# Starting the experts of the first ten chunks 36 edge tiles after their sums instead of 60, in a graph layer with a mixture of experts

## The chip, the core and the metric

The kernel runs on one core of one Trainium2 chip. The metric is the device time of one execution in microseconds. The core has five engines with a queue of instructions each: TensorE (PE in the profile; PEld is its loading of weights, which overlaps), VectorE (DVE), ScalarE (ACT), GpSimd (POOL) and SyncE (SP). An engine takes its instructions strictly in the order of the program, and waits when the next one needs something that isn't there yet.

## The reference

6,250 nodes with 256 features, 100,000 edges sorted by target. A graph layer adds to every node a linear map of itself and of the mean of its neighbours. Then a mixture of experts follows: 8 experts of 256-512-256, each node goes to the 2 with the highest scores.

```python
h = layernorm(x)
msg = segment_sum(h[src], dst); deg = segment_sum(1, dst)
x = x + concat([h, msg / max(deg, 1)]) @ W.T + b
xn = layernorm(layernorm(x)) * gamma + beta
logits = xn @ Wr + br;  top 2 of 8, w = softmax(top_vals)
for e in range(8):
    y += (gelu(xn @ W1[e] + b1[e]) @ W2[e] + b2[e]) * w_full[..., e]
x = x + y
```

## The kernel before

**Edges.** The edges are cut into 784 *edge tiles* of 128 edges. 14 tiles make a *window*, whose targets lie within 128 nodes; four windows (56 tiles) make a *chunk*; there are 14 chunks. For a tile, POOL gathers 128 rows of the transformed neighbours by an indirect DMA (L601, into 28 buffers `xg`, so that it can be 28 tiles ahead), DVE writes 0/1 matrices for half a window at a time (`hot`, L612), and PE multiplies the two and sums in PSUM (`pS`, L618). At a window's end ACT keeps a copy of the sums (`keep_sums`, L640), and DVE makes the nodes' new features of them (`window_x1`, L658 to L660).

**From sums to experts.** When the four windows of a chunk are done, a chain of small steps leads to its experts: DVE and ACT make the norms and the routing, PE counts the tokens of each expert (`count_tokens`, L678, which waits for DVE's `both`, L672), DVE writes matrices that sort the tokens (`one_hot_slots`, L697 and L698), PE sorts them (L705) and ACT takes them out of PSUM (L708). DVE works out where each expert's run of tokens goes (`share_runs`, `place_rest`, `place_runs`; the last result is `runs_i`, L780). Then ACT copies the runs into the experts' input `xe` in 32 copies (`copy_runs`, L859, 8 groups of 4). `find_rows` (a matmul at L809, then DVE to L822) makes a plan of where each node will find its results, and SP writes it to DRAM in four small DMAs (`put_plan`, L826) and reads back what is complete (`load_plans`, L841).

**Experts.** A chunk's experts are 16 *tasks* on PE: 8 of the first layer (`hidden`, L884, 16 recorded matmuls each, followed by 8 GELUs on ACT, L889) and 8 of the second (`result`, L897, 8 recorded matmuls each, followed by an addition on DVE, L901, and a DMA). Every first-layer task reads `xe`, and so waits for all of the chunk's copies. Tokens beyond 128 of an expert go to extra tiles, which are done once in each of three batches of chunks (chunks 1 to 8, 9 to 13, 14; `more_stages`, L927 to L945). When a batch is done, its nodes' results are gathered from DRAM (POOL, L976), weighted and added (DVE, L983) and written out.

**Who sets the order.** All of this is one stream, written out by hand. After each edge tile, `after` (L1085) issues what is due at that tile, and then tasks from a list: each task has a cost in the text (2.0 for a first-layer, 1.75 for a second-layer task), and a tile may spend 0.72 (0.6 in the last chunk). A chunk's 16 tasks cost 30, so they are spread over 42 tiles. What is due when is said by a class of offsets, counted in tiles from the chunk's last edge tile (`window_done`, L1014). There are three such classes, `Steps` (L993), `LateSteps` (L999) and `LastSteps` (L1005). Before the change chunks 1 to 10 use `Steps`, chunks 11 to 13 `LateSteps`, and chunk 14 `LastSteps`:

| step, offset in tiles | Steps | LateSteps |
| --- | --- | --- |
| features of the last window (x1) | 2 | 2 |
| norms, routing, choices | 9, 11, 16 | 7, 9, 13 |
| count | 19 | 15 |
| sorting matrices, from and to | 22, 28 | 17, 22 |
| sorting on PE, from and to | 26, 32 | 19, 25 |
| runs, rest, place | 30, 33, 36 | 20, 22, 24 |
| the 8 groups of copies, from and to | 40, 50 | 26, 34 |
| find_rows | 46 | 28 |
| put_plan, from and to | 47, 53 | 29, 32 |
| load_plans | 56 | 34 |
| experts start | 60 | 36 |

Offsets 1 to 56 are the tiles of the next chunk, 57 to 112 those of the chunk after it. So with `Steps` a chunk's tasks lie at offsets 60 to 102, inside the chunk after next, and with `LateSteps` at offsets 36 to 78, at the end of the next chunk and the start of the one after it.

Of the kernel before, what the change touches and what calls it, by code (L numbers as in the profile page):

```python
# [22 lines left out]
CW = 4  # L23
# [3 lines left out]
LATE = 40  # L27
XG = 28
RAW = 1
LATE_CHUNKS = 4  # L30


@with_exitstack
def gnn_ffn_kernel(ctx: ExitStack, tc: tile.TileContext, x, x_cols, src, dst, dst_next, gw, gw_t, gb, gb_cols, gamma, beta,
# [42 lines left out]
    W = src.shape[1]  # L77
# [545 lines left out]
    def take_raw_sums(V):  # L623
        V.raw = work.tile([P, D], F32, name="raw", bufs=1)
        nc.scalar.activation(V.raw, V.pS[:, :D], AF.Copy)
# [366 lines left out]
    now, spent, clock, due, added, spares = None, 0.0, 0.0, 0.0, 0.0, 0  # L992
    class Steps:  # L993

        x1, var, roots, norms, route, exps, weigh, choices, count = 2, 5, 7, 9, 11, 14, 15, 16, 19
        hot, sort = (22, 24, 26, 28), (26, 28, 30, 32)
        runs, rest, place, tiles, copied, rows, pace, start, apart = 30, 33, 36, 39, 40, 46, 1.5, 60, 2

    class LateSteps:  # L999

        x1, var, roots, norms, route, exps, weigh, choices, count = 2, 4, 5, 7, 9, 11, 12, 13, 15
        hot, sort = (17, 18, 20, 22), (19, 21, 23, 25)
        runs, rest, place, tiles, copied, rows, pace, start, apart = 20, 22, 24, 27, 26, 28, 1.25, 36, 1

    class LastSteps:  # L1005

        x1, var, roots, norms, route, exps, weigh, choices, count = 2, 4, 5, 6, 7, 8, 9, 10, 12
        hot, sort = (13, 14, 17, 18), (15, 16, 19, 20)
        runs, rest, place, tiles, copied, rows, pace, start, apart = 15, 16, 19, 24, 21, 22, 1, 29, 1

    def at(t, f, *args):
        later.setdefault(max(t, now), []).append(lambda: f(*args))

    def window_done(V, G, K, t):  # L1014

        i = V.g - K.first
        S = LastSteps if K.first + CW == W else LateSteps if K.first + LATE_CHUNKS * CW >= W else Steps
        G.x1.append(V.x1)
        more = 0
        if V.g < RAW:  # L1020
            take_raw_sums(V)
            at(t + 1, turn_raw_sums, V)
            at(t + 3, multiply_raw_sums, V)
            more = 4
        if V.g < W - 1:
            at(t + more, keep_sums, V)
        at(t + S.x1 + more, window_x1, V)
        at(t + S.x1 + more, statistics, G.mv[:, i, :], V.x1[:, :D])
        if i < CW - 1:
            return  # L1030
        at(t + S.var, variances, G)
        at(t + S.roots, roots, G)
        at(t + S.norms, norms, G, work)
        at(t + S.norms, logits, G)
        at(t + S.route, route, G, work)
        at(t + S.exps, exps, G)
        at(t + S.weigh, weigh, G, work)
        at(t + S.choices, choices, G)
        at(t + S.count, count_tokens, G, K)
        G.one_hot = [None] * CW  # L1040
        for m in range(CW):
            at(t + S.hot[m], one_hot_slots, G, m)
            at(t + S.sort[m], sort_tokens, G, m)
        at(t + S.runs, share_runs, K)
        at(t + S.rest, place_rest, K)
        at(t + S.place, place_runs, K)
        at(t + S.tiles, tile_experts, K)
        for e in range(NX):
            at(t + S.copied + int(e * S.pace), copy_runs, K, e)
        at(t + S.rows, find_rows, K)  # L1050
        for m in range(CW):
            at(t + S.rows + 1 + m * S.apart, put_plan, G, m)
        at(t + S.rows + 2 + CW * S.apart, load_plans, K)
        at(t + S.start, start_experts, K)
# [61 lines left out]
    for index in range(W // CW):  # L1116
        K = Group()
# [9 lines left out]
        for g in range(K.first, K.first + CW):  # L1127
            if g > 0:
                V = V_next
            for c in range(C):  # L1130
                t = g * C + c
                add_edges(V, c)
                if c == 0:
                    hot_tiles(V, HC)
                if c == HC and g + 1 < W:
                    V_next = new_window(g + 1, V)
                if t + XG < len(edge_tiles):
                    gather(*edge_tiles[t + XG])
                for to, what in loads[:1]:
                    loads.pop(0)  # L1140
                    nc.sync.dma_start(to, what)
                if u_tasks and t % 2 == 0:
                    u_tasks.pop(0)()
                    if not u_tasks:
                        u_pools.close()
                        slots = fast_pools.enter_context(tc.tile_pool(name="slots", bufs=2))
                        at(t + 60, load_last)
                        xe = slots.tile([P, KD, SC], F32, name="xe", bufs=1)
                        for n in range(4):
                            at(t + 3 + 5 * n, clear_slots, n)  # L1150
                        w1_sb, w2_sb, parts = weights(slots)
                        for n, (to, what) in enumerate(parts):
                            at(t + 2 + 2 * n, nc.scalar.dma_start, to, what)
                if c == HC + 5:
                    load_u(V)
                if c == C - 1:
                    window_done(V, G, K, t)
                after(t)
# [12 lines left out]
    with tc.If(wrong_r > 0), tc.tile_pool(name="gp", bufs=1) as gp:  # L1171
# [9 lines left out]
        with tc.For_i(0, W * C) as j:  # L1181
# [16 lines left out]
            count = gp.tile([P, 1], F32, name="count")  # L1198
# [113 lines left out]
```

## Time and profile before

| | |
| --- | --- |
| three timed runs | median 1427.65 us (1426.55 to 1431.58) |
| the profiled execution's own time | 1418.08 us |
| its span, first to last instruction | 1416.3 us |
| first edge tile starts, last one ends | 101.0 and 1255.8 us |
| mean granted clock of TensorE | 0.892 of full speed |
| POOL's gather of one edge tile (L601) | 0.951 us mean, and 0.30 us until the next at its fastest |

Times in the profile are microseconds from the start of the span. A timeline line gives start, length, engine, line of the code, operation, tiles, how many instructions were merged (xN), and in brackets the idle time of the engine before it and what ended that. A line by stretches gives for each engine its busy time and, in parentheses, its instructions, then the granted clock of TensorE, the DMAs' share and their rate. One matmul of the text appears as two records, since the numbers are float32.

### The profile page before, as it was taken

The page shows a single profiled execution, that of the slowest core. Times are in us where ns is not written, and L with a number is a line of the kernel's source. Part 1 is how long each engine was busy: PE and PEld are TensorE (multiplying, and loading weights), DVE is VectorE, ACT ScalarE, POOL GpSimd, SP SyncE. Part 2 cuts the span into 40 slices and gives each one's busy share as a digit, 9 for nine tenths or more (in the row PEclk, how much of TensorE's full clock was granted, in tenths as well). Part 3 has the DMA queues.
Part 4 walks back from the last instruction along what each step waited for, and adds up shares of the span by engine and source line. Part 5 has one row for each costly group of instructions (what it writes and reads, how often), then busy time and mean ns, then how long its engine had stood idle before and what let it go on. Part 6 is the DMA issues. An engine that isn't in the chain of part 4 may idle for free. (4 is left out here: it accounts for less than half of the span.)

```text
span 1416.3 us, 18881 instructions
## 1 busy us (share of the span) xinstructions
PE 1123.6 (79%) x5352; PEld 903.0 (64%) x5352; DVE 690.8 (49%) x2433; ACT 460.5 (33%) x1281; POOL 843.9 (60%) x892
## 2 busy tenths in 40 slices
PE   7819957696987879698796969899889897986760
PEld 6718734575766758586675857567767786774650
DVE  6637776163444435354443534555462643656423
ACT  3310003333342333344243323433542343532310
POOL 0256666666666666666666666566656666564543
PEclk9859977898998989899897988999999998997876
DMA  9858895445454454544445454454545453564754
GB/s 331 285 181 269 270 324 157 104 123 122 114 128 113 114 120 117 123 122 120 118 115 112 123 119 115 118 124 115 120 111 133 116 134 103 115 197 139 197 148 126
DMA packets 143578, 210.08 MB, mean 148 GB/s; under 512 B 36652, under 2 KB 111128, under 8 KB 143340
## 3 DMA queue, kind: packets, MB, share of 16 engines
q0 software_dynamic: 42768, 118.91, 34.3%
q1 hardware_dynamic: 92364, 80.45, 18.0%
q10 hardware_dynamic: 8336, 9.45, 2.0%
q8 instruction: 45, 0.74, 0.2%
q14 instruction: 65, 0.53, 0.1%
HBM read 163.86 MB, written 44.86 MB: 147 GB/s over the span
## 5 line engine op out<-in xcount | busy, mean ns | idle before, releaser
L601 POOL DMA_INDIRECT xg<-z_d,src_i x770 | 732.5, 951 | 415.2 <-issue 175.7
L618 PE MATMUL pS<-xg,hot 128*128 128x265 f32 x1568 | 452.4, 418 | 68.8 <-DVE hot L612 33.4
L618 PEld LDWEIGHTS pS<-xg,hot 128*128 128x128 f32 x1568 | 304.8, 204 | 151.7 <-issue 97.5
L884 PE MATMUL ph<-xe,w_sb 128*128 128x128 f32 x1792 | 255.4, 293 | 75.5 <-issue 66.3
L884 PEld LDWEIGHTS ph<-xe,w_sb 128*128 128x128 f32 x1792 | 243.1, 207 | 94.8 <-issue 77.4
L612 DVE TENSOR_TENSOR hot<-cols,rel 128x896 f32<-128x896 f32 x112 | 121.9, 1089 | 275.5 <-PE pS L618 154.3
L897 PE MATMUL py<-w_sb,hid 128*128 128x256 f32 x896 | 223.2, 391 | 28.0 <-issue 16.8
L889 ACT ACTIVATE hid<-ph,b_sb 128x128 f32<-128x128 f32 x448 | 126.4, 374 | 270.4 <-remote 125.5
L897 PEld LDWEIGHTS py<-w_sb,hid 128*128 128x128 f32 x896 | 172.2, 195 | 64.5 <-issue 36.4
L859 ACT ACTIVATE xe<-xs x448 | 139.3, 311 | 86.3 <-issue 36.4
L976 POOL DMA_INDIRECT xg<-y_d,plans x98 | 95.7, 977 | 83.1 <-issue 21.4
L901 DVE TENSOR_TENSOR rows<-py,b_sb 128x512 f32<-128x512 f32 x56 | 38.5, 688 | 168.9 <-PE py L897 62.7
L708 ACT ACTIVATE xs<-pm,beta_sb,gamma_sb 128x256 f32<-128x256 f32 x112 | 57.2, 566 | 169.2 <-PE pm L705 73.7
L705 PE MATMUL pm<-to,xn 128*128 128x256 f32 x224 | 62.5, 403 | 24.6 <-DVE to L698 18.7
L640 ACT ACTIVATE sums<-pS 128x265 f32<-128x265 f32 x55 | 21.4, 389 | 172.1 <-PE pS L618 100.2
L705 PEld LDWEIGHTS pm<-to,xn 128*128 128x128 f32 x224 | 44.1, 201 | 35.6 <-issue 11.6
L271 PE MATMUL ph<-gc,x_t 128*128 128x264 f32 (+1 forms) x200 | 58.8, 420 | 8.2 <-ACT root L180 4.2
L889 ACT ACT_TABLE_LOAD x25 | 32.1, 1283 | 77.8 <-PE pS L618 43.5
L271 PE MATMUL pm<-gc,x_t 128*128 128x264 f32 (+1 forms) x192 | 54.9, 411 | 0.0
L271 PEld LDWEIGHTS ph<-gc,x_t 128*128 128x128 f32 x200 | 40.2, 205 | 18.6 <-ACT root L180 4.6
L983 DVE SCALAR_TENSOR_TENSOR xg<-xg,plans,xg 128x256 f32<-128x256 f32 (+1 forms) x98 | 45.4, 482 | 12.5 <-DMA xg<-y_d,plans 10.9
L660 DVE SCALAR_TENSOR_TENSOR x<-pS,rdeg,x 128x264 f32<-128x264 f32 x55 | 27.1, 493 | 48.1 <-DMA x<-u_d 35.4
(214 smaller groups left out, 873.4 us busy)
## 6 DMA issues: line engine op xcount, KB each, us to landing
y_d<-rows SPq DMA_DIRECT2D x56, 256.0 KB
xg<-z_d,src_i POOLq DMA_INDIRECT x770
w_sb<-w_dram ACTq DMA_DIRECT2D x16, 512.0 KB
x<-u_d SPq DMA_DIRECT2D x55, 132.0 KB
x_d<-x SPq DMA_DIRECT2D x55, 128.0 KB
u_d<-u_t SPq DMA_DIRECT2D x24, 264.0 KB
x_t<-x_cols_dram SPq DMA_DIRECT2D x12, 512.0 KB
xu<-x_dram SPq DMA_DIRECT2D x24, 256.0 KB
```

What stands on the lines that cost most here:

```text
L271: nc.tensor.matmul(pz, x_t[:, t, k, :], gc[:, h * KD + k, :n], start=(k == 0), stop=(k == KD - 1))
L601: nc.gpsimd.indirect_dma_start(out=xg[(g * C + c) % XG][:, :DZ], out_offset=None, in_=z_d[:, :], in_offset=bass.IndirectOffsetOnAxis(ap=sr ...
L612: nc.vector.tensor_tensor(hot, col[:, None, :].to_broadcast([P, HC, P]), V.rel[:, c:c + HC, None].to_broadcast([P, HC, P]), op=ALU.is_equal)
L618: nc.tensor.matmul(V.pS, V.hot[c // HC][:, c % HC, :], xg[(V.g * C + c) % XG], start=(c == 0), stop=(c == C - 1))
L705: nc.tensor.matmul(px[:, k, :], G.xn[i][:, k * P:(k + 1) * P], G.one_hot[i], start=True, stop=True)
L708: nc.scalar.activation(xs[:, at:at + 2 * P], px[:, k, :], AF.Identity, bias=beta_sb[:, k:k + 1], scale=gamma_sb[:, k:k + 1])
L859: nc.scalar.activation(xe[:, :, bass.ds(to_at, CAP)], src[:, :, bass.ds(src_at, CAP)], AF.Copy)
L884: nc.tensor.matmul(ph[:, i, a * SH:(a + 1) * SH], w1_sb[:, U.e + a, k, c * P:(c + 1) * P], xe[:, k, at:at + SH], start=(k == 0), stop=(k = ...
L889: nc.scalar.activation(U.hid[:, c, a * SH:(a + 1) * SH], ph[:, i, a * SH:(a + 1) * SH], AF.Gelu, bias=b1_sb[:, U.e + a, c:c + 1])
L897: nc.tensor.matmul(U.py[:, h, :], U.hid[:, c, h * P:(h + 1) * P], w2_sb[:, U.e + h, c, :], start=(c == 0), stop=(c == KH - 1))
L976: nc.gpsimd.indirect_dma_start(out=V.y2[r], out_offset=None, in_=y_d[:K.batch.end_row, :], in_offset=bass.IndirectOffsetOnAxis(ap=plans[:c ...
L983: nc.vector.scalar_tensor_tensor(V.o, V.y2[r], plans.bitcast(F32)[:count, n, 2 + r:3 + r], V.o, op0=ALU.mult, op1=ALU.add)
```

## The change

The class `Steps` takes over the offsets of `LateSteps`, which goes, with the constant that chose between them. So chunks 1 to 10 go through the same steps as chunks 11 to 13 do; chunks 11 to 14 keep theirs. No instruction's shape changes, and the number of matmuls, gathers, DVE instructions and DMAs stays the same.

```diff
-LATE_CHUNKS = 4
...
     class Steps:
-        x1, var, roots, norms, route, exps, weigh, choices, count = 2, 5, 7, 9, 11, 14, 15, 16, 19
-        hot, sort = (22, 24, 26, 28), (26, 28, 30, 32)
-        runs, rest, place, tiles, copied, rows, pace, start, apart = 30, 33, 36, 39, 40, 46, 1.5, 60, 2
-
-    class LateSteps:
-
         x1, var, roots, norms, route, exps, weigh, choices, count = 2, 4, 5, 7, 9, 11, 12, 13, 15
         hot, sort = (17, 18, 20, 22), (19, 21, 23, 25)
         runs, rest, place, tiles, copied, rows, pace, start, apart = 20, 22, 24, 27, 26, 28, 1.25, 36, 1
...
-        S = LastSteps if K.first + CW == W else LateSteps if K.first + LATE_CHUNKS * CW >= W else Steps
+        S = LastSteps if K.first + CW == W else Steps
```

## Prediction

> **What bounds the kernel now.** I read first the busy times, then the stretches of the edge chunks, then the timelines of PE, ACT and DVE around one chunk's way from its sums to its experts.
>
> ```profile
> PE 1123.6 (79%) x5352; PEld 903.0 (64%) x5352; DVE 690.8 (49%) x2433; ACT 460.5 (33%) x1281; POOL 843.9 (60%) x892
> ```
>
> PE is the fullest engine, and it is the one that every edge tile and every task goes through in order. POOL is no bound: gathers start 1.25 us apart at the fastest (0.95 and 0.30), so 56 need 70 us, and PE's list of waits has only 1.7 us for a gather in the whole edge phase. So the time is PE's work plus PE's standing still. The stretches of chunks 8 and 9 (`Steps`), 12 and 13 (`LateSteps`):
>
> ```profile
> 667.20:750.60 83.40, 68.87 (x334) 56.03 (x334) 37.66 (x134) 30.58 (x86) 53.10 (x57) 0.91 0.48 117
> 750.60:832.60 82.00, 68.34 (x335) 56.41 (x335) 37.82 (x135) 28.61 (x80) 53.37 (x57) 0.90 0.48 119
> ...
> 1008.70:1096.60 87.90, 76.83 (x399) 64.59 (x399) 38.92 (x136) 31.95 (x90) 54.95 (x59) 0.94 0.48 120
> 1096.60:1179.50 82.90, 74.33 (x407) 62.36 (x406) 38.26 (x135) 33.09 (x94) 51.68 (x55) 0.96 0.47 120
> ```
>
> A usual chunk has 334 PE records, 69 us busy, 82 to 83 us long: 14 us idle, at a granted clock of 0.9. The late chunks look better (9 to 11 us idle, clock 0.95), but they hold 65 and 73 records more, because a backlog of tasks leaves PE no tile without one. So they are not yet proof of what `LateSteps` does to chunks with nothing left over.
>
> Where the 14 us go in a usual chunk, by PE's timeline:
>
> ```profile
> 826.71 2.05 PE L618 MATMUL pS<-xg,hot 128*128 128x265 f32 x8
> 832.56 3.48 PE L618 MATMUL pS<-xg,hot 128*128 128x265 f32 x8 [3.80 <-issue]
> 835.83 2.24 PE L884 MATMUL ph<-xe,w_sb 128*128 128x128 f32 x16
> ...
> 841.67 0.27 PE L884 MATMUL ph<-xe,w_sb 128*128 128x128 f32 x1 [1.83 <-issue]
> 843.78 0.37 PE L884 MATMUL ph<-xe,w_sb 128*128 128x128 f32 x1 [1.84 <-issue]
> 845.89 0.60 PE L884 MATMUL ph<-xe,w_sb 128*128 128x128 f32 x2 [1.73 <-issue]
> ```
>
> Some 3.8 us go at tile 56, where PE has raced through tiles without tasks and DVE's next `hot` ends only at 832.5. The larger part is a *crawl* from 839 to 852: single matmuls 0.7 to 1.8 us apart with no semaphore missing, 9 us lost. It comes again in chunks 3 to 10, each time while SP writes the plan (here 831 to 846) and POOL issues gathers back to back. It does not come beside the `LateSteps` plans at 1060, 1144 and 1227 (at most single gaps of a microsecond), when PE had tasks all along. Its cause I can't read from the trace.
>
> **The change, step by step.** The cycle of a usual chunk is the time from one start of experts to the next. First matmuls of L884 are at 253.4 (chunk 1) and 835.8 (chunk 8): seven cycles of 83.2 us. I build the new cycle from three legs and compare.
>
> *Leg 1, start of experts (offset 36) to the chunk's end (56).* 21 tiles at 0.46 us (two records of 0.225 apart) are 9.7; by 0.72 a tile, six first-layer tasks (1.78 each at full clock, from 1216.82 to the next start in PE's timeline of chunk 14's edges) and two second-layer ones (1.72, from 1221.55) fall here, 14.1; two joins of windows (L621, 0.55) 1.1. Together 24.9. As PE has stood still before, I add 2: after 3.80 us idle above, 8 records took 3.48 us instead of 2.05. Leg 1 is 27.
>
> The Trainium skill ("TensorE: Matmul & The Clock Gate", the table "Why this matters for your kernels") says that gaps over about 3 us bring the array back to half clock, and this speaks against gathering the idle time in one place. The row above agrees; by the page's window of 3.4 us the loss would be about 1.7 us an occurrence (an estimate), against the 2 that I take from the row.
>
> *Leg 2, the chunk's end to count (offset 15).* PE's own work is 17.4 (14 tiles 6.4, four second-layer and two first-layer tasks 10.4, one join), but the chain sums, x1, norms, routing, choices is longer: in chunks 11, 12 and 13 the first L678 started 21.2, 22.5 and 25.1 us after the chunk's last edge matmul (at 1030.15, 1117.58, 1204.80). I take their mean, 22.9. This is shorter than 39 us in chunk 8 (746.7 to 786.1), which has the crawl in it and four tiles more.
>
> *Leg 3, count to start (offset 36).* DVE needs count, four pairs of sorting matrices and some 35 small steps up to `runs_i`; in chunk 13 that went from 1205.9 to 1221.6 nearly without a pause. ACT then does 32 copies, all of which the first expert matmul waits for. In chunk 13, ACT and PE (two timelines):
>
> ```profile
> 1222.38 1.34 ACT L859 ACTIVATE xe<-xs  x4
> ...
> 1234.73 1.34 ACT L859 ACTIVATE xe<-xs  x4 [0.41 <-ACT xe L859]
> ```
> ```profile
> 1204.80 0.69 PE L678 MATMUL pm<-both,ones 128*128 128x64 f32 x2 [4.73 <-DVE both L672]
> ...
> 1236.12 2.05 PE L884 MATMUL ph<-xe,w_sb 128*128 128x128 f32 x16 [0.91 <-ACT xe L859]
> ```
>
> That is 31.3 us, 13.7 of it copies, and PE waited only 0.9 because tasks were left over from before. In chunks 2 to 8 after the change the last task is issued at about offset 20, so PE has 21 tiles (9.7), sorting (four times 0.87), two second-layer tasks (3.4), count, plan and join (1.8): 18.4 us of work in a leg of 31.3. **It will stand still 13 us in front of the first L884.** In the old order the same wait hardly shows, since 41 tiles and most tasks lie between count and start.
>
> Cycle: 27 + 22.9 + 31.3 and 0.8 for small waits for `rows` and `hid` (the 0.5 to 1.2 us a chunk of now) = 82.0, against 83.2, if there is no crawl. *The crawl* is the unknown. It costs 0 to 10 us (late chunks, chunk 9). The plan is now written from about 18 us after count on; POOL, refilling for the tiles that PE races through, is back to back just then. Most of it falls in PE's wait; what outlasts that, or slows ACT's copies, counts. I take 3, nearer to the late rows. Cycle 85.0; seven cycles cost 7 x 1.8 = **+12.6**.
>
> SP's queue: behind the plan's writes stand `load_plans`, the next x1's store and the next load of `u_d`. Moved from offsets 47 to 56 to 29 to 34, they no longer hold up the chunk's last x1, which now comes 18 us late after the crawl and comes 3.6 to 8.8 us after the end in chunks 11 to 13; that is in leg 2 already. POOL and DVE get no more instructions; nodes of the first batch are gathered 24 tiles earlier, and end before the last chunk in both.
>
> *Around the cycles.*
> - Chunk 1's experts start earlier: its count is held by DVE at 208.6 (13.1 us of wait in the trace) and will be; plus 31.3 is 239.9 instead of 253.4. **-13.5.** The weights are issued by 222 at the latest, and hide.
> - From the start of chunk 8's experts on there are 24 more tiles to go: 24 x 0.46 = **+11.0**; the crawl of chunk 9 (9.1 us of gaps) moves in front of that start: **-9.1**.
> - Batch 1's extra tiles keep PE in tasks until about tile 693. Then chunks 12 and 13 meet an empty list before their start, which they don't now (today's backlog ends where they start): 13 and about 7, **+20**.
> - Two tasks of each kind (7.0 us) come ahead of the last edge tile instead of behind it. From 1256 on PE's gaps before its last matmul add up to 37 us, so I count half as saved there: 7.0 - 3.5 = **+3.5**.
>
> Sum: 12.6 - 13.5 + 11.0 - 9.1 + 20 + 3.5 = +24.5. On the profiled execution's 1418.1 that is 1442.6; the median of the timed runs stands 9.6 above it, and I add the same 24.5 to it: **1452 us**.
>
> **Rivals.**
> 1. *The late rhythm without crawl and with a shorter chain (faster).* With few tasks in leg 3, DVE and ACT are less disturbed, and idle PE costs nothing where POOL refills. For it: no crawl in three of three `LateSteps` plans. Leg 1 at 25.5, leg 2 at 20.8, leg 3 at 30, and 1 for the rest make a cycle of 77.3 to 80, say 79: 7 x -4.2 = -29; if the two empty lists cost 12 instead of 20, around the cycles is +4: -25, 1402. It decides from a cycle of 81.5 down, where the sum turns negative. Against it: leg 3 has shown 31.3, 36.7 and 39.7, never 30.
> 2. *It cancels (within 0.5%).* Cycle 82.0 without crawl: 7 x -1.2 + 11.9 = +3.5, 1431.
> 3. *The crawl stays and hits ACT's copies.* They come with register loads, eight groups, and now lie in the middle of the plan's writing; a cycle of 92 gives 7 x 8.8 + 11.9 = +73, 1501. For it: chunks 3 to 10 crawled every time when POOL ran back to back. Against: copies that met its start (830.75, 832.56) kept their pace.
>
> **How the numbers follow.** Forecast 0.42 (+8 to +50), rival 1 0.25, rival 2 0.18, rival 3 0.15. A measurement of this kernel tells about 0.5% (7 us) from no change, so faster 0.25, same 0.18, slower 0.57. The range for 8 in 10 reaches into rivals 1 and 3: 1408 to 1490. Forecasts of slower alone: 1436 to 1478.
>
> **What would show it.** PE's waits for `xe` of L859 in front of L884 grow from a few single ones to one of 10 to 13 us in each of chunks 2 to 8, 12 and 13; waits named "issue" at L884 shrink from about 8 us a chunk to 3. First L884 at about 240, then every 85 us. The start of chunk 8's experts is then at 835 as before, with 24 tiles more behind it. Wrong if there is no such wait for `xe`; if the crawl is gone and starts are under 81 apart (faster); if copies take 20 us or more (rival 3).

## The result, and the profile after

The changed kernel takes 1508.72 us (median of four runs, 1490.90 to 1520.65), the kernel before, beside it, 1429.62 us. The ratio is 1.049, with an interval of 1.036 to 1.062; the highest of the four was a disturbed execution and is not in the ratio. The profiled execution takes 1505.28 us, its span is 1503.4. So the change costs 5% where the forecast had 1.7% (24.5 of 1418.1), and the time lies above the range.

The changed kernel has one class of steps less, so its line numbers are lower by one: L617 are the edge tiles, L883 the experts' first layer, L896 the second, L858 the copies, L677 the count. Busy times of the page:

```profile
PE 1139.6 (76%) x5352; PEld 908.7 (60%) x5352; DVE 689.8 (46%) x2433; ACT 461.4 (31%) x1280; POOL 846.9 (56%) x892
```

PE has the same 5,352 records, 16 us more work and 87 us more span: most of the loss is idle time. By stretches, chunks 8, 9, 12 and 13 of the changed kernel:

```profile
719.10:808.50 89.40, 69.60 (x336) 55.57 (x334) 37.87 (x134) 29.94 (x84) 53.90 (x57) 0.87 0.42 109
808.50:897.50 89.00, 70.08 (x336) 56.35 (x335) 37.44 (x135) 29.79 (x83) 52.58 (x57) 0.87 0.44 110
1080.00:1166.30 86.30, 76.02 (x400) 63.21 (x401) 37.95 (x135) 32.58 (x97) 53.04 (x57) 0.94 0.47 117
1166.30:1255.90 89.60, 69.27 (x336) 55.33 (x335) 37.91 (x134) 29.91 (x84) 52.54 (x56) 0.89 0.42 109
```

Usual chunks have grown by 6 to 7 us; chunk 13, which had 407 records in 82.9 us, now has 336 in 89.6. What PE waits for, in the list of waits of the changed kernel (total, times, longest, in us):

```profile
PE ph L883 <- ACT xe L858: 81.2, 10, 13.4
PE pS L617 <- issue: 49.2, 16, 28.0
PE ph L883 <- issue: 46.1, 54, 10.7
```

The first line is new: ten waits for the copies, in front of first expert matmuls, which were some 5 us in all before. The third was 66.3 before. Two single gaps under the name issue are no crawl: the 28.0 stands in front of the first edge tile (the trace of the kernel before puts the same gap down to DVE's `hot`), and the 10.7 is an eleventh wait for copies, in front of chunk 2's experts, since the last copy ends at 328.6 and the matmul starts at 328.7. The new wait and the crawl are seen in PE's timeline of chunk 9 of the changed kernel:

```profile
820.69 0.40 PE L883 MATMUL ph<-xe,w_sb 128*128 128x128 f32 x2 [0.82 <-issue]
822.14 0.39 PE L883 MATMUL ph<-xe,w_sb 128*128 128x128 f32 x2 [1.04 <-issue]
823.59 0.40 PE L883 MATMUL ph<-xe,w_sb 128*128 128x128 f32 x2 [1.07 <-issue]
...
853.16 0.38 PE L808 MATMUL pm<-row_f,ones 1*128 1x32 f32 x2 [1.60 <-DVE row_f L774]
853.47 5.08 PE L617 MATMUL pS<-xg,hot 128*128 128x265 f32 x14
862.13 1.25 PE L617 MATMUL pS<-xg,hot 128*128 128x265 f32 x2 [3.59 <-DVE rdeg L657]
870.73 3.79 PE L883 MATMUL ph<-xe,w_sb 128*128 128x128 f32 x16 [7.34 <-ACT xe L858]
```

The crawl is still there (the task at 818.6 to 826.1 takes 7.5 us, where a task takes 1.95), and the new wait begins 37 us behind it. The crawl is in ACT's copies too, in the same chunk:

```profile
857.70 1.34 ACT L858 ACTIVATE xe<-xs  x4 [0.42 <-issue]
...
862.83 0.31 ACT L858 ACTIVATE xe<-xs  x1 [0.95 <-issue]
863.60 0.31 ACT L858 ACTIVATE xe<-xs  x1 [0.46 <-ACT xe L858]
865.10 0.73 ACT L858 ACTIVATE xe<-xs  x2 [1.18 <-issue]
```

A group of four copies takes 1.34 us; here the fifth and the sixth group come in five pieces, with gaps of 0.5 to 1.2 us.

### The profile page after: what moved, and what is told of

The parts are those of the page before. It is cut to its first block, busy times and chain, and to the rows that moved or that the text cites. A ratio compares the mean times of both kernels' runs of the same rounds, so it can differ in the third digit from the quotient of the medians.

```text
span 1503.4 us, 18890 instructions
## 1 busy us (share of the span) xinstructions
PE 1139.6 (76%) x5352; PEld 908.7 (60%) x5352; DVE 689.8 (46%) x2433; ACT 461.4 (31%) x1280; POOL 846.9 (56%) x892
## 2 busy tenths in 40 slices
DMA packets 143578, 210.08 MB, mean 140 GB/s; under 512 B 36652, under 2 KB 111128, under 8 KB 143340
## 4 chain that ended last, share of the span: by engine, by line
PE 51%; DVE 13%; issue 13%; ACT 8%; another core or an unknown queue 3%; DMA 3%; ACTq 3%; SPq 0%; POOL 0%; DVEq 0%; POOLq 0%
PE pS L617 17%; PE ph L883 15%; PE py L896 11%; ACT xe L858 5%; PE pm L704 2%; PE py L944 2%; PE pS L620 2%; ACTq L847 2%; DMA u_d<-u_t 1%; PE ph L926 1%; DVE hot L611 1%; DMA xg<-y_d,plans 1%; DVE xg L982 1%; ACTq L858 1%
## 5 line engine op out<-in xcount | busy, mean ns | idle before, releaser
L617 PE MATMUL pS<-xg,hot 128*128 128x265 f32 x1568 | 451.5, 415 | 68.9 <-issue 49.2
L617 PEld LDWEIGHTS pS<-xg,hot 128*128 128x128 f32 x1568 | 303.9, 204 | 146.1 <-issue 74.8
L883 PE MATMUL ph<-xe,w_sb 128*128 128x128 f32 x1792 | 258.9, 298 | 130.1 <-ACT xe L858 81.2
L883 PEld LDWEIGHTS ph<-xe,w_sb 128*128 128x128 f32 x1792 | 244.2, 210 | 157.5 <-ACT xe L858 87.1
L896 PE MATMUL py<-w_sb,hid 128*128 128x256 f32 x896 | 229.9, 400 | 19.7 <-issue 14.5
L896 PEld LDWEIGHTS py<-w_sb,hid 128*128 128x128 f32 x896 | 178.3, 201 | 55.9 <-issue 28.7
L858 ACT ACTIVATE xe<-xs x448 | 139.3, 311 | 94.6 <-issue 42.8
L975 POOL DMA_INDIRECT xg<-y_d,plans x98 | 95.6, 976 | 91.2 <-DVE xg L982 24.5
L329 POOL DMA_INDIRECT xg<-x_dram,src_i x14 | 13.5, 961 | 61.4 <-DMA src_i<-src_dram 57.4
```

The lines of the kernel that those rows point to most:

```text
L617: nc.tensor.matmul(V.pS, V.hot[c // HC][:, c % HC, :], xg[(V.g * C + c) % XG], start=(c == 0), stop=(c == C - 1))
L858: nc.scalar.activation(xe[:, :, bass.ds(to_at, CAP)], src[:, :, bass.ds(src_at, CAP)], AF.Copy)
L883: nc.tensor.matmul(ph[:, i, a * SH:(a + 1) * SH], w1_sb[:, U.e + a, k, c * P:(c + 1) * P], xe[:, k, at:at + SH], start=(k == 0), stop=(k = ...
L896: nc.tensor.matmul(U.py[:, h, :], U.hid[:, c, h * P:(h + 1) * P], w2_sb[:, U.e + h, c, :], start=(c == 0), stop=(c == KH - 1))
L975: nc.gpsimd.indirect_dma_start(out=V.y2[r], out_offset=None, in_=y_d[:K.batch.end_row, :], in_offset=bass.IndirectOffsetOnAxis(ap=plans[:c ...
```

## The experiments

**The question.** My theory after the result: the price is the chain from a chunk's sums to its copies, which now ends last in each cycle, and the crawl is alike in both kernels. The rival: the change calls up a crawl of its own, since the plan is now written beside the copies.

The runs came in four rounds (e, f, g and h), which differ by the crawl. In f and h the kernel before takes 1428 to 1430 us, as in all that was shown so far, in e and g 1197 to 1199. I call these *crawling* and *quiet* chips, but the name says no more than what the round showed: the record numbers the chips of the four rounds 2, 8, 3 and 2, so number 2 was quiet in the first round and crawling in the last, 28 minutes later. Each ratio is to the kernel before on the same chip, beside it, with its 95% interval. The expectations of round e were written for a crawling chip and met a quiet one, so their microseconds can't be compared with what was measured.

**1. The changed kernel again** (unaltered), on a crawling and on a quiet chip.

> The changed kernel, unaltered, beside the kernel before on whatever chip this is. Where the kernel before needs 1197 us (the chip of the first four experiments, on which its cycles are 70 us and no crawl shows): Theory A, cycles 77 to 79 and 1305 to 1320 us, as with the plan under the tasks, since without a crawl the plan's place does not matter; theory C (the plan's writes matter): 1330 or more. Where it needs 1430: 1505.

> The changed kernel, unaltered. Theory A (the wait for the copies is the price of the change, and the crawl is a matter of the chip, alike in both kernels): on a chip where the kernel before takes about 1430 us, 1.050; on one where it takes about 1197 us, no crawl in either, the starts 78 us apart where the kernel before has 70, so 1.09 to 1.10. Theory B (the change calls up a crawl of its own, because the plan is written beside the copies): at 1197 us it gives 1.03 or less, since there is no crawl to call up.

Measured: 1499.89 us, 1.050 [1.044, 1.056], on the crawling chip; 1313.17 us, 1.0945 [1.091, 1.098], on the quiet one. PE's gaps over 0.4 us that the trace names issue sum to 92 us in the first run and to 0 in the second. (Of the 92, 27.6 are the gap in front of the first edge tile and 8.7 the wait for copies in front of chunk 12's experts; 56 are left.) So the change costs more where there is no crawl at all, 115 us, than where there is, 72. The rival is out as the cause of the loss: it allowed 1.03. On the quiet chip, PE's timeline of chunk 7 and its waits:

```profile
567.08 1.95 PE L883 MATMUL ph<-xe,w_sb 128*128 128x128 f32 x16
...
597.05 3.40 PE L617 MATMUL pS<-xg,hot 128*128 128x265 f32 x14
601.70 0.71 PE L617 MATMUL pS<-xg,hot 128*128 128x265 f32 x2 [1.25 <-DVE hot L611]
611.57 3.79 PE L883 MATMUL ph<-xe,w_sb 128*128 128x128 f32 x16 [9.16 <-ACT xe L858]
```
```profile
PE ph L883 <- ACT xe L858: 95.3, 11, 9.9
...
PE pm L808 <- DVE row_f L774: 14.0, 9, 1.6
PE pm L704 <- DVE to L697: 12.9, 12, 1.2
```

The task that crawled above takes 1.95, and the same wait stands in front of the first L883: 9 us a chunk.

**2. The early steps alone**: chunks 1 to 10 take the offsets of the change, but their experts start at 60 as before; chunks 11 to 14 are as before. Against the kernel before, in `Steps`:

```diff
-        x1, var, roots, norms, route, exps, weigh, choices, count = 2, 5, 7, 9, 11, 14, 15, 16, 19
-        hot, sort = (22, 24, 26, 28), (26, 28, 30, 32)
-        runs, rest, place, tiles, copied, rows, pace, start, apart = 30, 33, 36, 39, 40, 46, 1.5, 60, 2
+        x1, var, roots, norms, route, exps, weigh, choices, count = 2, 4, 5, 7, 9, 11, 12, 13, 15
+        hot, sort = (17, 18, 20, 22), (19, 21, 23, 25)
+        runs, rest, place, tiles, copied, rows, pace, start, apart = 20, 22, 24, 27, 26, 28, 1.25, 60, 1
```

> Chunks 1 to 10 take the early, close steps of the change (count at offset 15, copies 26 to 34, plan 29 to 34), but their experts start at offset 60 as in the kernel before; chunks 11 to 14 are as before. Theory A, the experts start too close behind ACT's copies: PE's waits for xe in front of the first layer's matmuls fall from 7 to 13 us a chunk to under 2, and with 41 tiles and most tasks between count and start again the loss of 75 us goes entirely; cycles of 72 to 82 us instead of 90, so 1340 to 1430 us, no slower than the kernel before. Theory B, the early steps themselves cost (closer together, and queued behind tasks on DVE and ACT): cycles stay at 87 to 90, 1480 to 1510 us. Theory C, the plan's small writes and the crawl make the loss: now the plan is written under tasks, so the crawl of about 9 us a chunk goes and with it 8 to 10 us of the cycle, 1340 to 1370 us; A alone, with the crawl still there, gives 1400 to 1430.

> All steps of chunks 1 to 10 as in the change, but the experts start at 60 as before. Theory A: the early steps cost nothing by themselves, 1.00 within 0.5% on either kind of chip. Theory B, where the kernel before takes about 1430 us: the early plan still crawls beside the copies, but nothing waits for the copies; some of the crawl moves under a full PE or away: 0.98 to 1.00. If the crawl went to where PE has tasks and vanished, 13 us a cycle would go, and the ratio would be 0.93.

> All steps of chunks 1 to 10 as in the change, experts start at 60. Where the kernel before takes about 1430 us: if the crawl belongs to the chip wherever the plan is written, 1.00 within 1%, with a similar sum of gaps named issue on PE (before 116 us of gaps over 0.4 us). If it is called up by writing the plan beside a PE without tasks, the place of the plan (offsets 29 to 32, again without tasks on PE but in another stretch) moves it and leaves the sum. Where the kernel before takes 1197 us: 1.00 as measured there.

Measured: 1.0018 [0.9995, 1.004] and 1.0012 [0.999, 1.003] on quiet chips, 1.0022 [0.999, 1.006] on a crawling one, where PE's issue gaps sum to 119 us (116 before). Within 0.6% early steps cost nothing and gain nothing. The loss lies in the start.

**3. Where the start lies.** As in 2 with `start` at 48 and at 42, and the old steps with `start` at 52 instead of 60 (there the chunk's nodes enter the list of sums in `load_plans`; in the kernel they do so when the experts start).

> As the run with the start at 60, but experts of chunks 1 to 10 start at offset 48, half way. Theory A: between count and start PE gets 12 more tiles and 8 to 9 us more of tasks, some 14 us, about what it waits for xe at a start of 36 (13 at most); so that wait shrinks to 0 to 3 us, and cycles are 74 to 82 us, 1350 to 1430 us. Theory B: as with the start at 36, 1480 to 1510 us. Theory C (crawl decides): the plan at 29 to 34 is now again written while PE is without tasks or nearly so (tasks end at offset 34), so some crawl stays, 1400 to 1450 us.

> The early steps of the change in chunks 1 to 10, experts' start at offset 42 (chunks 11 to 14 as before). Theory A: six tiles more give PE 2.8 us of tiles and 4.4 of tasks in front of the start, so the wait for xe falls from 9 to about 2 us a chunk, cycles 71 to 73; between the 1215 us of a start at 48 and the changed kernel's time: 1230 to 1255 us where the kernel before needs 1197. If the loss came with the early steps or with the plan, it would stay near the changed kernel's time.

> The kernel before with its late steps (count at 19, copies 40 to 50), but the experts of chunks 1 to 10 start at offset 52, two tiles behind the last copy, as in the change, instead of 60. Theory A, it is the work that PE has between count and start that decides: here 33 tiles, 15 us, and some 14 us of tasks, 35 us with sorting, against a chain of about 37 (copies until 37 us after count): a wait for xe of 2 to 5 us a chunk, cycles 70 to 74, 1195 to 1230 us where the kernel before needs 1197. Rival, that two tiles between last copy and start are too few whatever lies before: a wait as in the change, 9 us, cycles of 78, 1300 us.

Measured: 48 gives 1.0145 [1.011, 1.018] on a quiet chip, 42 gives 1.0105 [1.007, 1.014] on a crawling one, and the old steps from 52 on 1.0052 [1.002, 1.008] there. At 48 the cycles are those of before (61 to 71 us), and the loss lies behind the eighth start, where the experts of chunks 12 and 13 wait 4.0 and 9.4 us for copies. The last kernel has the longest waits of all, where I had expected 2 to 5 us a chunk:

```profile
PE ph L885 <- ACT xe L860: 95.7, 8, 15.5
```

96 us of waiting (L885 and L860 are L884 and L859 of the kernel before), and 7 us of loss: PE's issue gaps over 0.4 us are down from 116 to 58 (11.9 of these are one more wait for copies, in front of chunk 6's experts), and the starts come 84.1 us apart, where they came 83.2. A wait is not its cost; the distance from start to start is. None of these kernels beats the kernel before.

**4. Half of the copies**: those of every second expert are left out in chunks 1 to 13 of the changed kernel, in `copy_runs`.

```diff
+        if e % 2 == 1 and K.first + CW < W:
+            return
```

> The changed kernel, but in chunks 1 to 13 the copies of every second expert are left out (16 instead of 32 on ACT; that part of the experts' input stays as it was). Theory A, the chain count, DVE's steps, ACT's copies sets the start: 6.9 of 13.7 us of copies go, the wait for xe falls from 9 to about 2 us a chunk, cycles from 78 to 71 or 72, the time by 50 to 65 us against the changed kernel (1250 to 1262 where that needs 1313). Rival, something beside the copies (gathers, DVE) holds PE there: cycles stay above 75, less than 30 us gained.

> The changed kernel without the copies of every second expert in chunks 1 to 13 (their tokens' results are then wrong). Where the kernel before takes 1197 us: if the copies in front of the first expert matmul are on the chain to the end, half of 13.8 us goes in each of 7 to 10 chunks, the cycle falls from 78 to 71, the ratio from 1.094 to 1.03 to 1.05; if something else sets the cycle (the gathers' 70 us, or the chain in front of the copies having slack), under 20 us go and it stays above 1.075. Where the kernel before takes about 1430 us: 1.00 as measured there.

Measured, both on crawling chips: 1430.42 us, 1.001 [0.998, 1.004], and 1433.27 us, 1.003 [0.999, 1.007]. Against run 1 beside it, the first is 69 us shorter. PE's waits from the first start to the eighth, of the changed kernel in run 1 and then of this one (whose L885 and L860 are L883 and L858):

```profile
PE ph L883 <- ACT xe L858: 60.5, 8, 10.1
```
```profile
PE ph L885 <- ACT xe L860: 8.1, 4, 2.1
```

The cycle falls from 89.2 to 84.0 us, though ACT gave up only a part of its 208.87 us of work in these seven cycles (173.31 are left). That is 5.1 us of work a cycle for 5.2 us of cycle: the copies are on the path, in full. That this holds without a crawl has not been run.

**5. The plan elsewhere.** The kernel before with the plan at 65, 67, 69 and 71, read at 74, for chunks 1 to 10; and the changed kernel with the plan at 41 to 47 (41 for 65 in the edit), read at 50, for chunks 1 to 13. In both the nodes enter the list in `load_plans`.

```diff
+        plan, step = S.rows + 1, S.apart
+        if S is Steps:
+            plan, step = (65, 2)
         for m in range(CW):
-            at(t + S.rows + 1 + m * S.apart, put_plan, G, m)
-        at(t + S.rows + 2 + CW * S.apart, load_plans, K)
+            at(t + plan + m * step, put_plan, G, m)
+        at(t + plan + 1 + CW * step, load_plans, K)
```

> The kernel before (start at 60), but in chunks 1 to 10 the plan is written at offsets 65 to 71 and read back at 74, under the tasks, instead of 47 to 56. If the plan's small writes make the crawl when PE has no tasks and POOL gathers back to back: gaps called issue at the first layer's matmuls fall from 8 us a chunk to 3 or less, the last x1 of a chunk comes 4 to 8 us behind its end instead of 18, cycles fall from 83 to 74 to 78: 1370 to 1395 us. If POOL alone makes it: the crawl stays where it is, 1425 to 1440 us. If the writes make it wherever they stand: it moves to offsets 65 to 80, same time.

> The kernel before with the plan written at offsets 65 to 71 and read at 74, beside tasks, for chunks 1 to 10. Where the kernel before takes about 1430 us: if the crawl comes from the plan's writes beside a PE without tasks, it goes, up to 9 us of 83 a cycle: 0.94 to 0.97. If it belongs to the chip whatever is written, 1.00 within 0.5%. Where the kernel before takes 1197 us: 1.00, nothing to tell.

> The kernel before with the plan written at offsets 65 to 71 beside tasks, for chunks 1 to 10. Where the kernel before takes about 1430 us: plan theory, the crawl at 47 to 53 goes, 0.94 to 0.97, PE's issue gaps from 116 to under 50 us; chip theory, 1.00 within 0.5% and the gaps stay at 100 or more. Where it takes 1197 us: 1.00, nothing to tell.

> The changed kernel (start at 36), but in chunks 1 to 13 the plan is written at offsets 41 to 47 and read back at 50, under the tasks, instead of 29 to 34, when PE has no tasks, POOL gathers back to back and ACT copies. Theory A: the wait for xe stays near 10 us a chunk, because the copies' 14 us stay behind count and sorting; only what the crawl adds to ACT's copies (16 against 14 us) and the gaps called issue (4 us a chunk) can go, 3 to 6 us a cycle: 1455 to 1490 us. Theory C: the crawl is the loss; cycles fall to 80 to 82, 1420 to 1435 us. If the plan's writes have nothing to do with the crawl: no change, 1500 us.

> The changed kernel with the plan written at offsets 41, 43, 45 and 47 and read at 50, behind the start of the experts, for chunks 1 to 13. Where the kernel before takes about 1430 us, theory A (the crawl belongs to the chip and not to the plan) gives what the changed kernel gives, 1.04 to 1.055; theory B (the plan beside the copies is what crawls) takes the crawl out of the leg from count to start, 37 to about 32 us, six or seven cycles, 1.02 to 1.03. Where the kernel before takes 1197 us, both give 1.09 to 1.10, as there is no crawl.

> The changed kernel with the plan written at 41 to 47, behind the start of the experts. Where the kernel before takes about 1430 us: chip theory 1.04 to 1.055 with the leg from count to start at 36 to 37 us; plan theory 1.02 to 1.03 and this leg at 32 to 33. Where it takes 1197 us: 1.094 as measured there.

Measured, the kernel before: 1.0003 [0.998, 1.002] and 1.0012 [1.000, 1.003] on quiet chips, 1.0013 [0.999, 1.004] on a crawling one, with PE's issue gaps over 0.4 us at 130 us (116 with the plan in its old place). Its waits on the crawling chip, then those of the kernel before:

```profile
PE ph L885 <- issue: 63.9, 70, 2.6
PE pS L618 <- issue: 54.3, 28, 27.9
```
```profile
PE ph L884 <- issue: 66.3, 72, 2.5
PE pS L618 <- DVE hot L612: 33.4, 2, 28.6
PE pS L618 <- issue: 32.2, 20, 4.0
```

The 27.9 is the gap in front of the first edge tile, which the other trace names `hot` (28.6); without it 102 us stand beside 116. At the experts' matmuls the gaps are alike (63.9 and 66.3), and so is the time: the plan does not make the crawl in this kernel. The changed kernel: 1.096 [1.092, 1.100] and 1.094 [1.091, 1.097] on quiet chips, 1.037 [1.031, 1.043] on a crawling one. The last is lower than run 1 (1.050) and just under what I had expected of no effect; but its leg from count to start is 36.7 us where run 1 has 36.3, and its profiled span of 1499.1 us is above the 1488.8 of run 1. The two profiled executions can't settle it, being the second longest of five (1500.86 us) and the shortest of four (1490.62). If the later plan gives some of the loss back there, the trace does not show where, and I leave it open.

That the crawl doesn't need the plan shows in the changed kernel's SP queue as well, around the crawl of 818 to 826:

```profile
780.00 0.87 SPq L825 DMA_DIRECT2D plan_d<-plan  x2
782.03 0.40 SPq L840 DMA_DIRECT2D plans<-plan_d  x1
...
820.02 0.37 SPq L902 DMA_DIRECT2D y_d<-rows  x1
822.90 0.34 SPq L644 DMA_DIRECT2D x<-u_d  x1
```

The last plan was written some 37 us before this crawl.

## Why the prediction was wrong, point by point

The span, cut at the first start of experts, the eighth, and the last edge matmul (us; "forecast" is the prediction's own sum for that piece; its 7.0 of tasks lie ahead of the last edge, the 3.5 that it takes off behind it). For the kernel before on a quiet chip the run with the later plan stands in, as it takes the same time (1.0012):

| piece | before | after | difference | forecast | quiet: before | after | difference |
| --- | --- | --- | --- | --- | --- | --- | --- |
| to the first start | 253.4 | 240.2 | -13.2 | -13.5 | 225.4 | 222.0 | -3.4 |
| seven cycles | 582.4 | 630.5 | **+48.1** | +12.6 | 482.1 | 546.1 | +64.0 |
| to the last edge | 420.0 | 471.5 | **+51.5** | +28.9 | 354.9 | 412.6 | +57.7 |
| to the end | 160.5 | 161.2 | +0.7 | -3.5 | 134.6 | 133.6 | -1.0 |
| span | 1416.3 | 1503.4 | +87.1 | +24.5 | 1197.0 | 1314.3 | +117.3 |

The two middle pieces by stretches, first of the kernel before, then of the changed one:

```profile
253.40:835.80 582.40, 479.41 (x2338) 389.69 (x2339) 263.48 (x939) 209.15 (x575) 375.29 (x397) 0.91 0.48 118
835.80:1255.80 420.00, 368.89 (x1873) 300.58 (x1872) 195.67 (x687) 161.75 (x458) 261.19 (x277) 0.94 0.48 120
```
```profile
240.20:870.70 630.50, 485.04 (x2338) 390.20 (x2338) 262.49 (x939) 208.98 (x575) 373.58 (x393) 0.87 0.43 109
870.70:1342.20 471.50, 394.34 (x1940) 317.73 (x1941) 201.00 (x698) 162.82 (x460) 275.77 (x290) 0.91 0.44 112
```

and the seven cycles on quiet chips, of the kernel before with the later plan, then of the changed one:

```profile
225.40:707.50 482.10, 449.70 (x2339) 360.78 (x2340) 265.54 (x946) 211.87 (x576) 364.89 (x385) 0.98 0.57 140
```
```profile
222.00:768.10 546.10, 456.11 (x2339) 377.95 (x2339) 263.95 (x939) 209.63 (x575) 373.11 (x393) 0.92 0.50 126
```

*The wait came, somewhat shorter than forecast.* PE stands still in front of the first L883 of chunks 2 to 8, 12 and 13. I had 13 us each, and about 7 for chunk 13; on the crawling chip it is 6.9 to 13.4 for chunks 2 to 8 (9.6 on the mean), 7.2 and 10.5 for chunks 12 and 13, on the quiet one 9. The first start (240.2 for 239.9) came out by luck: its count stood at 205.9 where I had 208.6, and the leg from there took 34.3 us where I had 31.3. The half clock after the wait came too. 16 records in 3.79 us instead of 2.05 is 1.74 us in the first task, at a granted clock of 0.50 (from 870.73 to 874.50, and on the quiet chip from 611.57 to 615.36). The clock stays there for 3.0 to 6.2 us behind such a wait, so that 1.5 to 3.1 us are lost each time (an estimate: half of that stretch), 2.4 on the mean of chunks 2 to 8. I had put 2, and the prediction's estimate from the Trainium skill ("TensorE: Matmul & The Clock Gate", section "What's actually happening", by its window of 3.4 us) was 1.7, which is low.

*The step that failed is the crawl*: "Most of it falls in PE's wait; what outlasts that, or slows ACT's copies, counts. I take 3". Mean legs of chunks 2 to 8, and the mean of their seven cycles:

| | start to chunk's end | to count | to start | cycle |
| --- | --- | --- | --- | --- |
| forecast (crawl and small waits apart) | 27 | 22.9 | 31.3 | 82.0 and 3 |
| after, quiet chip | 27.0 | 18.1 | 32.9 | 78.0 |
| after, crawling chip | 26.7 | 26.2 | 37.2 | 90.1 |

Without a crawl the cycle is 78.0, less than my 82.0: the leg to count is 4.8 us shorter than the late chunks had shown. But the same instructions need 90.1 on the crawling chip. So the crawl costs 12.1 us a cycle where I had 3, 8.1 of them in the leg to count and 4.3 in the leg to the start. (This puts all that differs between the two kinds of chip down to the crawl. 4.1 of the 12.1 are busy time of PE, 485.0 us for 456.1 in the seven cycles, at a granted clock of 0.87 for 0.92; no run separates that from the gaps.) In the kernel before it costs at least 83.2 - 68.9 = 14.3 (on a quiet chip the gathers hold the cycle up): nearly all of it stayed, and I had compared a new cycle almost without it with an old one full of it.

It did not hide for a plain reason. A wait on PE hides only what PE loses beside the chain. The chain itself runs over PE (the task of 7.5 us at 818 lies between the chunk's end and count), DVE and ACT (copies 15.7 us instead of 13.9), and a crawl of any of them lengthens it. PE's own account of the seven cycles says so too: waits for copies +63 (with the 10.7 of chunk 2), issue gaps -42 (80 to 39), small waits for DVE and the rest +21, busy +6. I had foreseen the first two (at L883 the issue gaps fell to 3.3 us a chunk, where I had 3), and not that DVE's steps between count and start would stop PE for three more microseconds a chunk. On the quiet chip the account is the same with other names: waits for copies +64, waits for gathers -32 (all 31.7 gone), small waits for DVE +26, busy +6.

*The second failed term is what comes behind the eighth start*: up to the last edge +51.5 for 28.9. The four terms were 24 tiles (+11.0), the crawl of chunk 9 (-9.1), two empty lists (+20) and four tasks that come ahead of the last edge (+7.0). PE's waits for copies grew by 21.0, as said; but only 4.9 us of issue gaps went, waits for DVE and the rest grew by 10.0, and PE was busy 25.4 longer for 68 records more. These records are the 24 tiles (48 records, 11.0 us), two joins (4, 1.1 us) and a single first-layer task (16, 1.8 us): the four tasks were misread. The 11.5 us left of the 25.4 go with the lower granted clock (0.94 to 0.91), which no run separates. Behind the last edge, where I had taken 3.5 off, nothing came back (+0.7).

*POOL* was no bound, as said, on the chip of the prediction. On a quiet one it is: the kernel before (with the later plan) waits for gathers 50 times in its seven cycles, and its full cycles of 68 to 72 us are the 56 gathers of 1.25.

```profile
PE pS L618 <- DMA xg<-z_d,src_i: 31.7, 50, 1.4
```

*The rivals.* The third, with a cycle of 92 and 1501 us, describes the result best: the crawl stayed and reached the copies. But its sign, copies of 20 us or more, did not come (15.7 on the mean, 17.6 at most in chunks 2 to 8), and its reason, the plan's writing, is wrong for the kernel before and not borne out for the changed one, as part 5 shows. The first had 25.5, 20.8 and 30 for the legs, 76.3 in all; without a crawl they are 78.0, but there the kernel before has a cycle of 68.9.

## What to carry to other kernels

When a chain of steps over several engines feeds the next stage, the cycle is the work left between that stage's start and the end of the tiles that begin the next chain, plus the chain. With the start at 36 it is 27.0 + 51.0 = 78 us on a quiet chip against a floor of 70 by the gathers; each tile that the start moves back takes away 1.3 us (27 / 21), so by this estimate the change would cease to cost in the cycles at about 42. The run at 42 fits that, but on a crawling chip (83.2 us, as before); on a quiet one only 48 was run (67.8). And a disturbance that the old cycle contains belongs into the new one too, until a run shows it gone: subtract it from both or from neither.

## What was not expected of the hardware

- The same program takes 1197 us on some chips and 1428 us on others. The changed kernel was profiled on both kinds (spans of 1314.3 and 1503.4 us), with the same instructions and bytes (210 MB in 143,578 packets). On the crawling chips PE, ACT and SP advance for some microseconds in steps of 0.4 to 1.8 us without a missing semaphore (SP's four plan writes at 831 in the kernel before took 13.95 us). Two runs of the changed kernel crawl at nearly the same places: counted in PE's records, gaps over 0.4 us stand at 1531, 1536 and 1538 in one, at 1531, 1535 and 1536 in the other, and 333 to 334 records later again. That recurs with the chunk, and so does everything else in the program; what it is, no run here settles, nor whether it belongs to the chip or to the hour, for which the number 2 of two rounds speaks.
- A wait of 7.3 us (crawling chip) or 9.2 us (quiet chip) in front of a task costs 1.74 us more in the task itself (3.79 us instead of 2.05), at a granted clock of 0.50.
